# A transformer block in split 16-bit products: one pass of attention scores with DMA transposes in place of two passes

## The chip, the cores and the metric

The kernel runs on one core of one Trainium2 chip. The metric is the device time of one execution in microseconds (us), lower is better. A core has five engines that run beside each other, each in the order of its own instruction list: TensorE (PE, matrix products into PSUM, with weight loads shown as PEld), VectorE (DVE), ScalarE (ACT), GpSimd (POOL) and SyncE (SP), which here issues nearly all DMAs. They wait for one another through semaphores.

## The reference

```python
# x: (16, 512, 512); 16 heads of 32; INTER = 1408
xn = _layernorm(x)
def attn(x):
    qkv = jnp.einsum('bsd,ed->bse', x, w_qkv) + b_qkv           # q, k, v by heads
    scores = jnp.einsum('bhqd,bhkd->bhqk', q, k) / math.sqrt(Hd) + causal
    out = jnp.einsum('bhqk,bhkd->bhqd', jax.nn.softmax(scores), v)
    return jnp.einsum('bsd,ed->bse', out, w_out) + b_out
def ffn(x):                                                      # ternary weights with scales
    g = jnp.einsum('th,ih->ti', x, gate_w) * gate_s
    u = jnp.einsum('th,ih->ti', x, up_w) * up_s
    return jnp.einsum('ti,hi->th', jax.nn.silu(g) * u, down_w) * down_s
return x + attn(xn) + ffn(xn)
```

The ternary weights hold only -1, 0 and 1. All tensors are float32.

## The kernel before

A batch row has 512 tokens by 512 features. It is worked on in tiles of 128 partitions by 512: four token blocks (tb) or four feature chunks (kc). Float32 products are made from 16-bit ones: a value is split into a high and a low float16 half after an exact scaling, and high by high, high by low and low by high are summed in PSUM. Ternary weights need no split; they lie in SBUF as float16 (wg, wu, wd).

Attention goes by slots. A slot is a group of four heads of one row, so there are 16 x 4 = 64 slots. Two passes over the scores are made. The first (`s1_step`, L354 to L369) computes a head's 128 queries by all keys up to them, in PSUM tile s; VectorE takes the row maximum with the causal mask (L363, negm), and ScalarE the exponential in place, only for its row sum (L369, den). `s1_fin` then turns maxima and denominators into pieces of float16 (pc), transposes them on TensorE (mT, L409) and sends the maxima by a DMA into rows 96 to 98 of the query tile QS (L405). The second pass (`s2_step`) computes the scores again, this time with keys on partitions, with 99 rows so that the maximum is already subtracted (L426): ScalarE takes the exponential (p, L441), GpSimd zeroes what is above the diagonal (L436), ScalarE and VectorE write the high and low halves ph (L443) and pl (L446). These are the moving operands of the value products (`av_step`, L461), which are made in four places of the slot, one for each key block, each with three groups of four matmuls: one matmul a head, 32 columns of TensorE's array each. `av_fin` spreads the reciprocal denominators over partitions by four matmuls (R, L483), scales the result and splits it into oh and ol.

The dense products fill TensorE between these steps. A `Fill` lays them out evenly over a slot: the query and key projections two slots ahead (`qk_proj`), the transposes of the next row's norm (`ln_tr`, L276), the gate and up chunks (`ffn_chunk`), the value projection (`v_proj`), the down projection (`down_tile`) and the output projection of the row before (`out_tile`). They share `mm_group` (L213).

The order is written out by hand: `at(time, function)` gives every step a planned time in us, and `run_events` emits the steps sorted by it. TensorE and SyncE issue in exactly that order; the planned times order the work and say nothing of how long it takes. `qk_place` (L316) has six DMAs a slot, which copy the halves of queries and keys from (dim, head) partitions into QS and KS, of which there are two sets each. PSUM's eight banks are three for the dense products (mm), two for the first scores (s1), two for the second (s2), and one for the value products (av).

```python
    def place():
        nc.vector.tensor_copy(mT(), ps()[:80, :P])
        nc.sync.dma_start(QSt[slot][96:99].rearrange("p j (i c) -> p (j i) c", i=4), mT()[32:80])
```

## Time and profile before

| what | value |
|---|---|
| median of 3 runs | 2243.9 us (2239.43 to 2244.49) |
| span of the profiled execution, first to last instruction | 2242.9 us, 1.0 us under that median |
| busy: PE, DVE, ACT, POOL | 2161.9, 1768.9, 1646.2, 1004.2 us |
| granted TensorE clock, mean | 0.996 |
| DMA, mean over the span | 54 GB/s, 122.04 MB in all |
| share of 16 DMA engines, queue of SyncE and ScalarE | 21.6% |

The page of a profile has the busy time of each engine, the span in 40 slices (each digit a tenth of the slice), the DMA queues, the chain of work that ended last, and groups of instructions: line, engine, operation, output and inputs, count, busy time, mean in ns, and then the idle time of the engine just before them with what ended it. In the timeline a line begins with its start and its duration in us. SPq is SyncE's queue: the duration there is that of the issue, not of the transfer.

### The profile page before, as it was taken

What the parts mean: (1) busy time and instruction counts of PE and PEld (TensorE: products, weight loads), DVE (VectorE), ACT (ScalarE), POOL (GpSimd) and SP (SyncE); (2) the same over time, 40 slices, a digit from 0 to 9 for tenths busy, and PEclk for the clock granted to TensorE, in tenths of its full rate; (3) what the DMA queues carried; (4) which work ended last, traced back from release to release, by engine and by line L of the source; (5) the groups of instructions that cost most, each with busy time, mean ns of one, the idle gap of its engine ahead of it and who ended that gap; (6) DMA issues with size and microseconds to landing.
All of it is one profiled execution on the core that took longest, in us unless ns stands there. A gap on an engine that the chain in (4) does not pass through costs nothing.

```text
span 2242.9 us, 39079 instructions
## 1 busy us (share of the span) xinstructions
PE 2161.9 (96%) x12994; PEld 964.2 (43%) x12994; DVE 1768.9 (79%) x4748; ACT 1646.2 (73%) x4145; POOL 1004.2 (45%) x1299
## 2 busy tenths in 40 slices
PE   5899999999999999999999999999999999999998
PEld 2434444444444444444444444444444444444433
DVE  7887869788787877879778697887978878787774
ACT  4877868778677777767777687786777877777773
POOL 5444353543534444344443534435344353544434
PEclk9999999999999999999999999999999999999999
DMA  8122131121221222222222211213212222122111
GB/s 195 34 48 67 34 72 51 31 67 47 63 56 29 67 52 53 56 44 58 47 62 48 68 43 38 72 39 71 54 28 67 53 57 53 40 52 44 40 38 40
DMA packets 99251, 122.04 MB, mean 54 GB/s; under 512 B 13920, under 2 KB 68576, under 8 KB 99040
## 3 DMA queue, kind: packets, MB, share of 16 engines
q1 hardware_dynamic: 94416, 115.14, 21.6%
q0 software_dynamic: 4624, 4.33, 1.2%
q8 instruction: 104, 1.70, 0.3%
q14 instruction: 107, 0.88, 0.1%
HBM read 55.85 MB, written 16.78 MB: 32 GB/s over the span
## 4 chain that ended last, share of the span: by engine, by line
PE 48%; DVE 17%; ACT 16%; DMA 6%; POOL 6%; issue 4%; SPq 1%; POOLq 0%; ACTq 0%; DVEq 0%
PE u L213 7%; PE g L213 7%; PE v L213 6%; PE dn L213 5%; ACT s L369 5%; PE op L213 5%; PE av L461 5%; PE qk L213 5%; DMA xr<-in_x 4%; ACT ph L443 4%; PE s L354 4%; ACT p L441 4%; DVE pl L446 3%; PE s L426 3%; DVE s L363 3%
## 5 line engine op out<-in xcount | busy, mean ns | idle before, releaser
L446 DVE SCALAR_TENSOR_TENSOR pl<-p,ph 128x512 f16<-128x512 f32 (+1 forms) x704 | 530.6, 757 | 139.2 <-ACT ph L443 135.7
L369 ACT ACTIVATE s<-s,negm 128x128 f32<-128x128 f32 (+3 forms) x1024 | 514.8, 503 | 170.7 <-DVE negm L363 163.9
L363 DVE CUSTOM_DVE_ANT_0 s<-s,mask 128x128 f32<-128x128 f32 (+3 forms) x1024 | 501.9, 492 | 118.0 <-PE s L354 116.2
L436 POOL TENSOR_SCALAR_AFFINE_SELECT p<-p 128x128 f32<-128x128 f32 (+2 forms) x704 | 304.0, 433 | 617.4 <-ACT p L441 589.3
L443 ACT ACTIVATE ph<-p 128x512 f16<-128x512 f32 (+1 forms) x704 | 416.0, 595 | 128.6 <-POOL p L436 125.5
L441 ACT ACTIVATE p<-s 128x512 f32<-128x512 f32 (+1 forms) x704 | 394.5, 561 | 58.3 <-PE s L426 56.0
L354 PE MATMUL s<-KS,QS 96*128 96x128 f16 (+3 forms) x1024 | 308.1, 301 | 50.9 <-ACT s L369 36.7
L519 POOL TENSOR_TENSOR hl<-ft,hh 128x512 f16<-128x512 f32 x176 | 216.8, 1232 | 236.7 <-ACT hh L518 236.5
L213 PE MATMUL u<-xh,wu 128*128 128x512 f16 x704 | 268.4, 381 | 0.0
L213 PE MATMUL g<-xh,wg 128*128 128x512 f16 x704 | 267.9, 381 | 0.0
L213 PE MATMUL dn<-wd,hh 128*128 128x512 f16 x704 | 267.6, 380 | 0.0
L213 PE MATMUL g<-xl,wg 128*128 128x512 f16 x704 | 267.1, 379 | 0.0
L213 PE MATMUL u<-xl,wu 128*128 128x512 f16 x704 | 266.8, 379 | 0.0
L213 PE MATMUL dn<-wd,hl 128*128 128x512 f16 x704 | 266.2, 378 | 0.0
L426 PE MATMUL s<-QS,KS 99*128 99x512 f16 (+3 forms) x1024 | 255.1, 300 | 0.5 <-DMA QS<-mTs 0.5
L369 ACT ACTIVATION_READ_ACCUMULATOR s<-s,negm 128x1 f32 x1024 | 209.7, 205 | 0.0
L213 PEld LDWEIGHTS <-wu 128*128 128x128 f16 x1408 | 126.4, 97 | 156.5 <-issue 31.2
L213 PEld LDWEIGHTS <-wg 128*128 128x128 f16 x1408 | 130.4, 98 | 143.1 <-issue 16.1
L306 POOL TENSOR_TENSOR qkl<-qkt,qkh 128x512 f16<-128x512 f32 x128 | 156.9, 1226 | 64.6 <-DVE qkh L305 52.5
L354 PEld LDWEIGHTS <-QS 96*128 96x128 f16 x1024 | 99.8, 97 | 140.1 <-issue 40.0
L518 ACT CAST hh<-ft 128x512 f16<-128x512 f32 x176 | 108.0, 614 | 59.7 <-DVE ft L516 57.9
L213 PEld LDWEIGHTS <-wq_h 128*128 128x128 f16 x1024 | 97.2, 97 | 122.8 <-issue 15.9
(131 smaller groups left out, 3508.0 us busy)
## 6 DMA issues: line engine op xcount, KB each, us to landing
xc<-in_x SPq DMA_DIRECT2D x64, 256.0 KB
QS<-qkh SPq DMA_DIRECT2D x128, 128.0 KB
KS<-qkh SPq DMA_DIRECT2D x128, 128.0 KB
xr<-in_x SPq DMA_DIRECT2D x64, 256.0 KB
out<-y SPq DMA_DIRECT2D x64, 256.0 KB
QS<-qkl SPq DMA_DIRECT2D x64, 128.0 KB
KS<-qkl SPq DMA_DIRECT2D x64, 128.0 KB
wq<-in_wqkvP SPq DMA_DIRECT2D x12, 256.0 KB
```

The lines of the kernel that those rows point to most:

```text
L213: nc.tensor.matmul(ps(), l, r, start=(k == 0), stop=(k == n - 1))
L306: f.after(1.8, lambda: nc.gpsimd.tensor_tensor(l(), t(), h(), ALU.subtract))
L354: nc.tensor.matmul(ps()[:, :n], QSt[slot][0:96, j, i * P : (i + 1) * P], KSt[slot][0:96, j, 0:n], start=True, stop=True,)
L363: last["rowmax"] = nc.vector.tensor_tensor_reduce(ps()[:, :n], ps()[:, :n], mask[:, 512 - n :], -(2.0 ** -7), 3e38, ALU.add, ALU.min, d["n ...
L369: nc.scalar.activation(ps()[:, :n], ps()[:, :n], AF.Exp, bias=d["negm"]()[:, c : c + 1], scale=-1.0, accum_out=d["den"]()[:, c : c + 1],)
L426: nc.tensor.matmul(ps()[:, u * n : (u + 1) * n], KSt[slot][0:KROW, j, kb * P : (kb + 1) * P], QSt[slot][0:KROW, j, kb * P : 512], start=Tr ...
L436: nc.gpsimd.affine_select(dg, dg, [[0, len(js)], [1, P]], ALU.is_ge, 0.0, base=0, channel_multiplier=-1)
L441: at(when + 0.35, lambda: nc.scalar.activation(p32()[:, :w], ps()[:, :w], AF.Exp, scale=2.0 ** -7))
L443: at(when + 1.5, lambda: nc.scalar.mul(ph()[:, :w], p32()[:, :w], 2.0 ** 15))
L446: lambda: nc.vector.scalar_tensor_tensor(pl()[:, :w], p32()[:, :w], 2.0 ** 15, ph()[:, :w], ALU.mult, ALU.subtract),
L461: nc.tensor.matmul(d["av"]()[j * 32 : (j + 1) * 32, kb * P : 512], st[b][vn]()[:, kb, f : f + 32], d[("p", kb, j)][pi](), start=(kb == 0 a ...
L519: f.after(2.0, lambda: nc.gpsimd.tensor_tensor(hl(), t(), hh(), ALU.subtract))
```

## The change

The scores are computed once. `score_pair` takes two heads and one query block: each head's scores go into one of four PSUM banks (s1), the row maximum and the exponential in place follow as before, and now the exponentials are kept. VectorE takes the reciprocals of the two row sums, GpSimd scales them, ScalarE writes the high half of the normalized weights from PSUM (`high`) and VectorE the low half (`low`), both into pq in SBUF, queries on partitions. One DMA transpose on SyncE (`turn`) puts all 128x128 blocks of the pair (4, 8, 12 or 16) with keys on partitions into pT, of which there is one set. The value products of a group are one run of 72 matmuls in the next slot, `AV_LAG` = 7.0 us of planned time after its start, and `av_fin` only splits their result. The second score pass, the pieces of maxima, the spread and the causal select are gone, and with them the rows 96 to 98.

The norm's rows are split into halves with tokens on partitions (ScalarE, GpSimd) and put on feature partitions by two DMA transposes a token block, in place of TensorE transposes. The query and key projections run one slot ahead instead of two. The ternary weights lie in SBUF as one-byte floats. A slot's planned length is the dense work + 4.4 instead of + 7.4.

```diff
-    QSt = [cp.tile([P, 4, 512], F16, name=f"QS{n}") for n in range(NS)]
-    KSt = [cp.tile([P, 4, 512], F16, name=f"KS{n}") for n in range(NS)]
-    for n in range(NS):
-        # rows 96..98 = 2^13, 2^2, 2^-9
-        nc.gpsimd.memset(KSt[n][96:99], 2.0 ** -9)
-        nc.gpsimd.memset(KSt[n][96:98], 4.0)
-        nc.gpsimd.memset(KSt[n][96:97], 8192.0)
+    QSt = [cp.tile([96, 4, 512], F16, name=f"QS{n}") for n in range(NS)]
+    KSt = [cp.tile([96, 4, 512], F16, name=f"KS{n}") for n in range(NS)]
+    pT = [
+        cp.tile([P, 2, 4, 2, 2, 256], F16, name="pT23"),
+        cp.tile([P, 2, 2, 2, 2, 256], F16, name="pT01"),
+    ]
...
-    wg = cp.tile([P, KC, I], F16, name="wg")
-    wu = cp.tile([P, KC, I], F16, name="wu")
-    wd = cp.tile([P, IC, D], F16, name="wd")
+    wg = cp.tile([P, KC, I], F8, name="wg")
+    wu = cp.tile([P, KC, I], F8, name="wu")
+    wd = cp.tile([P, IC, D], F8, name="wd")
...
     def ln_norm(b, tb):
         s = st[b]
         xc = s["xs"][tb]
+        if tb == 0:
+            s["xh"] = wk.tile([P, KC, 512], F16, tag="xh", name=f"xh_{b}", bufs=2)
+            s["xl"] = wk.tile([P, KC, 512], F16, tag="xl", name=f"xl_{b}", bufs=2)
+        h = wk.tile([P, 512], F16, tag="xnh", name=f"xnh_{b}_{tb}", bufs=1)
+        l = wk.tile([P, 512], F16, tag="xnl", name=f"xnl_{b}_{tb}", bufs=1)
         nc.vector.tensor_scalar(
             xc, xc, s["mv"][:, tb, 0:1], s["rstd"][:, tb : tb + 1], ALU.subtract, ALU.mult
         )
-    def ln_tr(f, b, kc):
+        nc.scalar.copy(h, xc)
+        nc.gpsimd.tensor_tensor(l, xc, h, ALU.subtract)
+        s[("xn", tb)] = h, l
+    def ln_tr(b, tb):
         s = st[b]
-        ps = Lazy(lambda: mm(f"lnT_{b}_{kc}"))
-        def tr():
-            if kc == 0:
-                s["xh"] = wk.tile([P, KC, 512], F16, tag="xh", name=f"xh_{b}", bufs=2)
-                s["xl"] = wk.tile([P, KC, 512], F16, tag="xl", name=f"xl_{b}", bufs=2)
-            for tb in range(NT):
-                nc.tensor.transpose(
-                    ps()[:, tb * P : (tb + 1) * P], s["xs"][tb][:, kc * P : (kc + 1) * P], ident
-                )
-        f.pe(0.45, tr)
-        f.after(0.3, lambda: nc.scalar.copy(s["xh"][:, kc, :], ps()))
-        f.after(1.0, lambda: nc.vector.tensor_tensor(s["xl"][:, kc, :], ps(), s["xh"][:, kc, :], ALU.subtract))
...
+    def score_pair(when, gap, b, g, i, pr):
         slot = (b * NG + g) % NS
         n = (i + 1) * P
+        nm = f"{b}_{g}_{i}_{pr}"
+        den = Lazy(lambda: wk.tile([P, 2], F32, tag="den", name="den_" + nm, bufs=4))
+        r = Lazy(lambda: wk.tile([P, 2], F32, tag="r", name="r_" + nm, bufs=4))
+        pq = Lazy(lambda: wk.tile([P, 4, 2, 2, P], F16, tag="pq", name="pq_" + nm, bufs=3))
+        pss = []
+        def score(ps, j):
             nc.tensor.matmul(
                 ps()[:, :n],
+                QSt[slot][:, j, i * P : (i + 1) * P],
+                KSt[slot][:, j, 0:n],
                 start=True,
                 stop=True,
             )
+        def rowmax(ps, negm):
             last["rowmax"] = nc.vector.tensor_tensor_reduce(
+                ps()[:, :n], ps()[:, :n], mask[:, 512 - n :], -(2.0 ** -7), 3e38, ALU.add, ALU.min, negm()
             )
+        def expo(ps, negm, u):
             nc.scalar.activation(
+                ps()[:, :n], ps()[:, :n], AF.Exp, bias=negm(), scale=-1.0, accum_out=den()[:, u : u + 1]
             )
+        def recip():
+            nc.vector.reciprocal(r(), den())
+            nc.gpsimd.tensor_scalar(r(), r(), 2.0 ** 15, None, ALU.mult)
+        def half(u):
+            return [pq()[:, 0 : i + 1, u, z, :] for z in range(2)]
+        def high(ps, u):
+            nc.scalar.mul(half(u)[0], ps()[:, :n].rearrange("p (k q) -> p k q", q=P), r()[:, u : u + 1])
+        def low(ps, u):
+            h, l = half(u)
+            nc.vector.scalar_tensor_tensor(
+                l, ps()[:, :n].rearrange("p (k q) -> p k q", q=P), r()[:, u : u + 1], h, ALU.mult, ALU.subtract
+            )
+        def turn():
+            dst = pT[0 if i > 1 else 1][:, pr].rearrange("p k u z q -> p (k u z) q")
+            src = pq().rearrange("p k u z q -> p (k u z q)")
+            nc.sync.dma_start_transpose(
+                dst[:, 0 : 4 * (i + 1), (i % 2) * P : (i % 2 + 1) * P], src[:, 0 : 4 * n]
+            )
+        for u in range(2):
+            t = when + gap * u
+            ps = Lazy(lambda u=u: pp.tile([P, 512], F32, tag="s1", name=f"s1_{nm}_{u}", bufs=4))
+            negm = Lazy(lambda u=u: wk.tile([P, 1], F32, tag="negm", name=f"negm_{nm}_{u}", bufs=6))
+            pss.append(ps)
+            at(t, score, ps, 2 * pr + u)
+            at(t + 0.35, rowmax, ps, negm)
+            at(t + 0.7 + 0.001 * n, expo, ps, negm, u)
+        at(t + 1.3 + 0.002 * n, recip)
+        for u in range(2):
+            w = t + 1.8 + (0.002 + 0.001 * u) * n + 0.2 * u
+            at(w, high, pss[u], u)
+            at(w + 0.3 + 0.001 * n, low, pss[u], u)
+        at(t + 2.5 + 0.005 * n, turn)
...
+    def av_step(when, b, g):
         d = grp[(b, g)]
+        def run():
+            for side, k0 in ((0, 0), (1, 0), (0, 1), (1, 1), (0, 2), (0, 3)):
+                q0 = P if (side == 0 and k0 == 3) or (side == 1 and k0 == 1) else 0
+                col = 0 if side else 256
+                for x, (vn, z) in enumerate((("vh", 0), ("vl", 0), ("vh", 1))):
+                    for j in range(4):
+                        f = g * P + j * 32
+                        nc.tensor.matmul(
+                            d["av"]()[j * 32 : (j + 1) * 32, col + q0 : col + 256],
+                            st[b][vn]()[:, k0, f : f + 32],
+                            pT[side][:, j // 2, k0, j % 2, z, q0:256],
+                            start=(side == 0 and k0 == 0 and x == 0),
+                            stop=(k0 == 3 and x == 2),
+                            skip_group_check=True,
+                        )
+        at(when, run)
...
     def av_fin(when, b, g):
         d = grp[(b, g)]
         nm = f"{b}_{g}"
-        R = Lazy(lambda: pp.tile([P, 512], F32, tag="s2", name="R_" + nm, bufs=2))
-        r = Lazy(lambda: tmp32("Rs_" + nm, "r32", 1))
         oh = Lazy(lambda: wk.tile([P, 512], F16, tag="oh", name="oh_" + nm, bufs=5))
         ol = Lazy(lambda: wk.tile([P, 512], F16, tag="ol", name="ol_" + nm, bufs=5))
-        def spread():
-            for i in range(4):
-                nc.tensor.matmul(R()[:, i * P : (i + 1) * P], sel[:, i, :], d["rT"], start=True, stop=True)
-        at(when - 1.3, spread)
-        at(when - 0.9, lambda: nc.scalar.copy(r(), R()))
+        at(when, lambda: nc.scalar.mul(oh(), d["av"](), 2.0 ** -15))
         at(
-            when + 0.3,
-            lambda: nc.vector.scalar_tensor_tensor(r(), d["av"](), 2.0 ** -24, r(), ALU.mult, ALU.mult),
-        )
-        at(when + 1.2, lambda: nc.scalar.copy(oh(), r()))
-        at(when + 1.9, lambda: nc.gpsimd.tensor_tensor(ol(), r(), oh(), ALU.subtract))
+            when + 0.7,
+            lambda: nc.vector.scalar_tensor_tensor(ol(), d["av"](), 2.0 ** -15, oh(), ALU.mult, ALU.subtract),
+        )
         st[b][("o", g)] = (oh, ol)
...
     def attention_slot(s, t0, T):
+        if s > 0:
+            b, g = divmod(s - 1, NG)
+            at_av = t0 + AV_LAG
+            av_step(at_av, b, g)
+            av_fin(at_av + 2.2, b, g)
+        if s < NSLOT:
+            b, g = divmod(s, NG)
+            grp[(b, g)] = dict(
+                av=Lazy(lambda: pp.tile([P, 512], F32, tag="av", name=f"av_{b}_{g}", bufs=1)),
+            )
+            unit = T / (4 * sum((i + 1) * P + 150 for i in range(4)))
+            t = t0
+            for i in (3, 2, 1, 0):
+                gap = ((i + 1) * P + 150) * unit
+                for pr in range(2):
+                    score_pair(t, gap, b, g, i, pr)
+                    t += 2 * gap
...
+    AV_LAG = 7.0
     for s in range(NSLOT):
         b, g = divmod(s, NG)
         f = fillers(s)
-        T = f.total + 7.4
+        T = f.total + 4.4
         attention_slot(s, start, T)
         f.place(start, T)
...
-                at(start + T * (0.79 + 0.06 * tb), late, ln_norm, b + 1, tb)
+                at(start + T * (0.8 + 0.2 * tb), late, ln_norm, b + 1, tb)
+                at(start + T * (0.8 + 0.2 * tb) + 4.0, ln_tr, b + 1, tb)
```

## The prediction

> **What bounds the kernel now.** I read the shares of busy time, then the slices, the groups, the timeline of two stretches and the chain.
>
> ```profile
> span 2242.9 us, 39079 instructions
> PE 2161.9 (96%) x12994; PEld 964.2 (43%) x12994; DVE 1768.9 (79%) x4748; ACT 1646.2 (73%) x4145; POOL 1004.2 (45%) x1299
> PE   5899999999999999999999999999999999999998
> PEclk9999999999999999999999999999999999999999
> ```
>
> TensorE has 81 us of idle in the whole span, most of it in the first two slices, at a full clock. So its stream of matmuls is the bound, and work taken out of it is worth its own length, as long as nothing else becomes longer. The groups show the second score pass and what hangs on it:
>
> ```profile
> L446 DVE SCALAR_TENSOR_TENSOR pl<-p,ph 128x512 f16<-128x512 f32 (+1 forms) x704 | 530.6, 757 | 139.2 <-ACT ph L443 135.7
> L436 POOL TENSOR_SCALAR_AFFINE_SELECT p<-p 128x128 f32<-128x128 f32 (+2 forms) x704 | 304.0, 433 | 617.4 <-ACT p L441 589.3
> L443 ACT ACTIVATE ph<-p 128x512 f16<-128x512 f32 (+1 forms) x704 | 416.0, 595 | 128.6 <-POOL p L436 125.5
> L441 ACT ACTIVATE p<-s 128x512 f32<-128x512 f32 (+1 forms) x704 | 394.5, 561 | 58.3 <-PE s L426 56.0
> L426 PE MATMUL s<-QS,KS 99*128 99x512 f16 (+3 forms) x1024 | 255.1, 300 | 0.5 <-DMA QS<-mTs 0.5
> ```
>
> A matmul's mean there is longer than its turn, since matmuls overlap. The turn is the distance between two starts in the timeline:
>
> ```profile
> 1001.17 0.38 PE L213 MATMUL dn<-wd,hh 128*128 128x512 f16 x1
> 1001.39 0.38 PE L213 MATMUL dn<-wd,hl 128*128 128x512 f16 x1
> ...
> 1006.65 0.39 PE L483 MATMUL R<-mTs,sel 32*128 32x128 f16 x4
> 1006.97 0.25 PE L409 MATMUL mT<-ident,pc 128*80 128x128 f16 x1
> 1007.06 0.38 PE L213 MATMUL dn<-wd,hh 128*128 128x512 f16 x1
> ```
>
> 512 columns take 0.216 us, the reciprocal spread (R) 0.32, the transposed maxima (mT) 0.09. SyncE's queue, on which the new work lands, is seen in the full timeline:
>
> ```profile
> 58.59 0.87 SPq L405 DMA_DIRECT2D QS<-mTs  x1
> ...
> 60.99 0.38 PE L426 MATMUL s<-QS,KS 99*128 99x512 f16 x1 [0.54 <-DMA QS<-mTs]
> ```
>
> From the start of an issue to its reader 2.4 us pass, so some 1.5 after the issue. The placements of queries and keys (L316) hold the queue 0.55 to 0.61 us each, the loads of x 0.46 (four in 1.84).
>
> In the chain, the same step of a row (the load of xc behind the norm) recurs at 361.42 and ten rows later at 1728.37: 136.7 us a row, 34.2 a slot of four heads. 64 slots are 2187, the two ends 56. The profiled span is 1.0 us under the median of the runs, 2243.9; I add that at the end.
>
> [...] The trace holds no transpose by DMA and no one-byte matmul[...].
>
> **The change, part by part, per slot.**
>
> TensorE. Gone: the second scores, 4 x (0.216 + 0.167 + 0.11 + 0.055) = 2.2 us (turns of 512, 384, 256 and 128 columns at L426); R and mT 0.41; the norm's transposes, four in 0.44 to 0.50 us, 1.9 a row, 0.5 a slot. The value products (L461): now twelve groups of four in four places, each entered and left with 0.1 us lost; the four stretches I measured are 1.30, 0.97, 0.73 and 0.58 = 3.6 us. Then 18 groups in one run: 12 of 256 columns at 0.12 and 6 of 128 at 0.07, plus one switch 0.2, = 2.1. Saved 1.5. Together 4.6 us, 294 in all: 2161.9 falls to 1868, 29.2 a slot.
>
> VectorE. Gone: pl 530.6, the eight steps on maxima and denominators 107.5, the copy of mT 13.8, the norm's xl 43.8. Added: 1024 low halves from PSUM; by the nearest PSUM rows (688 ns for 512; 559, 424 and 294 from the row maxima) 256 x 1.965 = 503; 512 reciprocals between 0.15 and 0.25 us, taken 0.2: 102. The weight checks lose 27 reductions and gain 35, nothing. 1769 becomes 1678, 26.2 a slot: below TensorE, though not by much.
>
> ScalarE. Gone: 394.5 + 416.0 + 37.4 (copy of R). Added: 1024 high halves at 598, 495, 392 and 289 ns (p's two shapes, then their slope): 454. 1646 becomes 1252, 19.6 a slot, free. GpSimd: minus 304.0 (causal) and 75.0 (ol), plus 64 norm halves at 1.23 and 512 small products of 0.1 to 0.2: about 770, 12 a slot. But each small product now stands between a pair's exponentials and its high halves, and can sit behind one 1.23 us subtraction.
>
> SyncE, the part that decides. A group turns 2 x (4+3+2+1) x 4 = 80 blocks of 128x128[...], in eight DMAs[...]. Six placements at 0.59: 3.5; loads and stores 12 a row at 0.45: 1.4; weight checks 0.2. Sum 29.1 us in a slot in which TensorE needs 29.2. Gone is QS<-mTs, 0.76. The data themselves are 2.9 MB a slot[...]. [...]
>
> The new wait: pT is single. A group's first transpose waits until the value products of the group before have read pT, and those wait for that group's last transpose. Behind the waiting transpose SyncE holds the placements, loads and stores; behind them stand the next slot's scores (KS, QS). So a cycle is the queue's 29.1, plus 1.5 us until the last transpose has landed, plus 2.1 of products, less some 0.6 of loads or norm transposes that fit between: 32.1 us. That is 3 us over TensorE's stream, which the 4.6 saved pay for.
>
> One-byte weights: no time on TensorE; half the start-up load of 4.3 MB on the software queue, hidden behind the first row. Ends: the norm's halves now go through DMA at the start (+3), the last products wait for their transposes (+3), the first norm transposes (4.1) and the second projection (5.2) leave the start: 53 to 55. Sum: 64 x 32.1 + 55 = 2109, and 1 around the span: **2110 us**.
>
> **The rivals.**
>
> The transpose costs more a tile (slower). Break-even is 34.2 us a slot[...]. It would show as TensorE waiting in one block per slot for pT, or for KS.
>
> The four score banks (slower or level). A score tile now stays in PSUM from its matmul to its low half: at 512 columns 0.22 + 0.83 + 0.86 + 0.2 + 0.15 + 0.6 + 0.69 = 3.6 us plus the pair's second tile, and waits on a VectorE that is over 80% busy. Eight pairs through two places break even at 8.5 us a pair; I reckon 5 to 7. If this decides, 2250 to 2400.
>
> The queue is not the limit (faster still). [...] TensorE has 29.2 and about 1.3 us of waits: 64 x 30.5 + 55 = 2007; with no new wait at all 1925.
>
> That the change does not do what it says has nothing for it: the removed passes are gone from the code.
>
> **How the numbers follow.** The queue as summed, 2010 to 2230: 0.35. Queue not the limit, 1950 to 2010: 0.12. Within 0.3%, 7 us, which is what measurements of this kernel can tell from no change: 0.05. Dearer tiles 0.36, of which I leave 0.15 beyond 3300. Banks 0.12. Faster 0.47, same 0.05, slower 0.48: the sign is nearly open, since the forecast lies 130 us from the break-even of a price that no row shows. The likeliest case alone spans 2010 to 2230; the range that holds 8 in 10 goes from 1970 to 3300.
>
> **What would show it.** Right: no L426, R, mT or lnT in the groups; 29 us of TensorE stream a slot; SPq nearly full with transposes[...]; TensorE's idle some 3 us a slot, released by a DMA into pT. Wrong: a 16-block transpose of over 4.5 us from issue to issue (dearer tiles), idle of scores behind DVE pq (the banks), or TensorE at 96% again (the queue hidden).

## The result, and the profile after

The changed kernel takes 2335.24 us (median of 4 runs, 2322.34 to 2340.42) against 2242.07 us for the kernel before: 1.0407 times as long, 95% interval 1.0375 to 1.0439. The forecast was 2110 us and faster. The profiled execution took 2340.42 us, with a span of 2338.6. The page of the profile after, busy time and slices:

```profile
span 2338.6 us, 39976 instructions
PE 1978.5 (85%) x12930; PEld 926.2 (40%) x12930; DVE 1683.9 (72%) x4945; ACT 1408.0 (60%) x3697; POOL 775.2 (33%) x1101
PE   1978888988889888898888889898798898898886
PEclk9999999999999999999998999999999999999998
DMA  8567688788686787777786776876767777776774
```

No engine is full any more. TensorE, at 96% before, has 360 us of idle, spread over all slices, and a longer start (the first digit is 1, before it was 5). VectorE and GpSimd came out within 6 us of the prediction's sums (1678 and 770). The groups of the page say what TensorE waits for (after the bar: busy time and mean; then the idle time before the group, and what ended most of it):

```profile
L347 PE MATMUL s<-KS,QS 96*128 96x512 f16 (+3 forms) x1024 | 316.6, 310 | 279.1 <-DVE pq L377 278.0
L373 ACT ACTIVATE pq<-s,r 128x512 f16<-128x512 f32 (+3 forms) x1024 | 483.3, 524 | 297.9 <-POOL r L367 226.3
L471 POOL TENSOR_TENSOR xr<-xr,bo_b 128x512 f32<-128x512 f32 x64 | 81.2, 1269 | 198.2 <-DMA xr<-in_x 192.8
L205 PE MATMUL qk<-xh,wq_h 128*128 128x512 f16 x512 | 146.5, 412 | 47.4 <-DMA xh<-xnh 47.4
```

Read them as one chain. A score needs a PSUM bank, and a bank is free when VectorE has made the low half (L377). That waits for ScalarE's high half (L373), which waits for GpSimd's product of the reciprocal (L367). Ahead of some products in GpSimd's list stands the residual add L471, which has 198 us of idle, nearly all for the load of xr. The 278 us there are what the prediction named as the sign of the bank rival. The fourth line is the start: TensorE waits 47.4 us for the first norm rows.

The length of a slot is taken from the first score of one slot to that of the next. A row's four slots take 37.2, 33.8, 34.6 and 35.8 us after (means over slots 4 to 59), together 141.4; before, the same stretches of dense work (there they run beside the scores of the group after) take 35.5, 33.3, 34.4 and 33.4, together 136.6. So the slots cost 64 x (35.35 - 34.14) = 77 us more, and the two ends 19 more (76 against 58). The predicted 2109 had 32.1 a slot and 55.

One place where the chain is late, in the timeline of the kernel after, in slot 3 (the down projection); a line has its start, its duration, and in brackets the idle time before it with what ended it:

```profile
1039.40 0.54 SPq L470 DMA_DIRECT2D xr<-in_x  x1
...
1040.89 0.15 DVE L366 RECIPROCAL r<-den 128x2 f32<-128x2 f32 x1
...
1044.70 1.26 POOL L471 TENSOR_TENSOR xr<-xr,bo_b 128x512 f32<-128x512 f32 x1 [5.65 <-DMA xr<-in_x]
1045.93 0.21 POOL L367 TENSOR_SCALAR r<-r 128x2 f32<-128x2 f32 x1
1046.17 0.84 ACT L373 ACTIVATE pq<-s,r 128x256 f16<-128x256 f32 x2 [4.13 <-POOL r L367]
1046.68 0.88 DVE L377 SCALAR_TENSOR_TENSOR pq<-s,r,pq 128x256 f16<-128x256 f32 x2 [3.48 <-ACT pq L373]
1047.22 0.22 PE L347 MATMUL s<-KS,QS 96*128 96x128 f16 x1 [3.30 <-DVE pq L377]
```

The reciprocal is there at 1041.0; the product of 0.21 us comes at 1045.93, because the add before it waits for a load issued at 1039.40 that lands 5 us later. ScalarE, VectorE and at last TensorE stand. What this costs beside the 3.3 us is in the same kernel's busy time by stretches (busy us of PE, PEld, DVE, ACT, POOL, each with its count; granted clock, DMA share, GB/s):

```profile
1044.00:1048.00 4.00, 0.78 (x4) 0.31 (x4) 1.24 (x5) 1.34 (x5) 2.87 (x4) 0.92 0.41 85
1048.00:1052.00 4.00, 4.00 (x16) 1.75 (x15) 1.60 (x8) 2.19 (x9) 1.60 (x3) 0.65 1.03 219
```

After the gap TensorE is busy for all of the next 4 us, at a mean clock of 0.65. The clock records of the trace show half rate for 238.6 us in all after, and 19.6 before. All 46 half-rate stretches of after begin on one grid of 3.41 us, and nearly all last one or two of its steps (3.41 or 6.83 us). In the 3.41 us before these stretches TensorE is idle for 1.9 to 3.4 us (3.2 in the one shown), in one gap or in several: before the stretch at 1832.5 us there are two, of 1.00 and 0.86 us. The steps after the first score that no half rate follows have 2.0 us of idle at most. In the kernel before two of the three stretches follow a wholly idle step, and the third (at 2163.9 us) one with 1.33 us of idle, so the traces show no sharp limit. Part of the 1978.5 us of busy TensorE in after is slow work: it is busy in 197 of the 238.6 us, and there the dense 512-column matmuls start 0.427 us apart in place of 0.216 (medians), so about half of that, 99 us, is lost, which leaves 1880 where the prediction's sum was 1868.

### The profile page after: what moved, and what is told of

Read it like the earlier page. It is cut to its first block, busy times and chain, and to the rows that moved or that the text cites. A ratio compares the mean times of both kernels' runs of the same rounds, so it can differ in the third digit from the quotient of the medians.

```text
span 2338.6 us, 39976 instructions
## 1 busy us (share of the span) xinstructions
PE 1978.5 (85%) x12930; PEld 926.2 (40%) x12930; DVE 1683.9 (72%) x4945; ACT 1408.0 (60%) x3697; POOL 775.2 (33%) x1101
## 4 chain that ended last, share of the span: by engine, by line
PE 37%; DVE 24%; DMA 18%; ACT 6%; issue 6%; SPq 4%; POOL 4%; ACTq 0%; POOLq 0%; DVEq 0%
PE qk L205 11%; DMA pT<-pq 8%; DVE pq L377 7%; PE dn L205 6%; DMA xr<-in_x 5%; PE v L205 5%; DVE s L356 4%; PE u L205 4%; PE s L347 4%; PE g L205 4%; PE av L415 3%; ACT pq L373 3%; SPq L307 2%; DVE ft L459 2%; DVE ft L455 2%
## 5 line engine op out<-in xcount | busy, mean ns | idle before, releaser
L361 ACT ACTIVATE s<-s,negm 128x512 f32<-128x512 f32 (+3 forms) x1024 | 516.3, 504 | 362.2 <-DVE negm L356 313.6
L377 DVE SCALAR_TENSOR_TENSOR pq<-s,r,pq 128x512 f16<-128x512 f32 (+3 forms) x1024 | 524.8, 545 | 207.8 <-ACT pq L373 206.6
L373 ACT ACTIVATE pq<-s,r 128x512 f16<-128x512 f32 (+3 forms) x1024 | 483.3, 524 | 297.9 <-POOL r L367 226.3
L356 DVE CUSTOM_DVE_ANT_0 s<-s,mask 128x512 f32<-128x512 f32 (+3 forms) x1024 | 503.3, 493 | 218.6 <-PE s L347 213.6
L347 PE MATMUL s<-KS,QS 96*128 96x512 f16 (+3 forms) x1024 | 316.6, 310 | 279.1 <-DVE pq L377 278.0
L367 POOL TENSOR_SCALAR r<-r 128x2 f32<-128x2 f32 x512 | 110.5, 216 | 620.5 <-DVE r L366 550.2
L205 PE MATMUL dn<-wd,hh 128*128 128x512 fp8e4 x704 | 283.9, 403 | 0.0
L205 PE MATMUL dn<-wd,hl 128*128 128x512 fp8e4 x704 | 281.9, 400 | 0.0
L205 PEld LDWEIGHTS <-wu 128*128 128x128 fp8e4 x1408 | 135.9, 98 | 200.7 <-issue 61.3
L205 PE MATMUL qk<-xh,wq_h 128*128 128x512 f16 x512 | 146.5, 412 | 47.4 <-DMA xh<-xnh 47.4
L471 POOL TENSOR_TENSOR xr<-xr,bo_b 128x512 f32<-128x512 f32 x64 | 81.2, 1269 | 198.2 <-DMA xr<-in_x 192.8
L205 PE MATMUL qk<-xl,wq_h 128*128 128x512 f16 x512 | 146.1, 412 | 0.0
```

What stands on the lines that cost most here:

```text
L205: nc.tensor.matmul(ps(), l, r, start=(k == 0), stop=(k == n - 1))
L347: nc.tensor.matmul(ps()[:, :n], QSt[slot][:, j, i * P : (i + 1) * P], KSt[slot][:, j, 0:n], start=True, stop=True,)
L356: last["rowmax"] = nc.vector.tensor_tensor_reduce(ps()[:, :n], ps()[:, :n], mask[:, 512 - n :], -(2.0 ** -7), 3e38, ALU.add, ALU.min, negm())
L361: nc.scalar.activation(ps()[:, :n], ps()[:, :n], AF.Exp, bias=negm(), scale=-1.0, accum_out=den()[:, u : u + 1])
L367: nc.gpsimd.tensor_scalar(r(), r(), 2.0 ** 15, None, ALU.mult)
L373: nc.scalar.mul(half(u)[0], ps()[:, :n].rearrange("p (k q) -> p k q", q=P), r()[:, u : u + 1])
```

## The experiments

A table first; the sections below refer to it. Medians in us, the ratio to the kernel before with its 95% interval, the start of the first score, the length of a row's slots 0 to 3, and the time at half clock, the last three from the trace of the profiled execution.

| kernel | median | ratio | first score | slots 0, 1, 2, 3 | half clock |
|---|---|---|---|---|---|
| before | 2242.07 | 1 | 37.7 | 35.5, 33.3, 34.4, 33.4 | 19.6 |
| after | 2335.24 | 1.0407 (1.0375 to 1.0439) | 68.8 | 37.2, 33.8, 34.6, 35.8 | 238.6 |
| e1_mul_dve | 2364.41 | 1.0542 (1.0524 to 1.0559) | 70.3 | 38.8, 34.6, 33.3, 35.9 | 225.7 |
| e2_one_block | 2235.11 | 0.9952 (0.9935 to 0.9970) | 68.9 | 35.7, 30.7, 32.7, 35.8 | 159.5 |
| e3_ln_pe | 2269.77 | 1.0117 (1.0100 to 1.0134) | 45.2 | 38.2, 32.5, 32.2, 35.7 | 157.6 |
| e4_before_fp8 | 2251.83 | 1.0045 (1.0031 to 1.0060) | 35.9 | 36.5, 33.3, 34.4, 33.3 | 12.8 |
| e5_norm_slot3 | 2213.17 | 0.9870 (0.9854 to 0.9887) | 44.6 | 32.8, 31.6, 32.2, 37.5 | 101.1 |
| e6_xr_two | 2292.07 | 1.0217 (1.0200 to 1.0234) | 70.4 | 36.5, 33.6, 34.3, 34.4 | 208.4 |
| e7_both | 2231.51 | 0.9956 (0.9939 to 0.9973) | 45.5 | 32.8, 31.6, 32.3, 38.2 | |
| e8_both_mul_dve | 2243.80 | 1.0012 (1.0000 to 1.0025) | 45.6 | 33.9, 31.7, 32.6, 37.4 | |
| e9_add_late | 2232.12 | 0.9960 (0.9947 to 0.9974) | 45.9 | 33.2, 31.6, 32.2, 38.3 | |
| e10_after_add_late | 2297.31 | 1.0250 (1.0229 to 1.0271) | 69.5 | 36.2, 33.3, 33.9, 34.5 | |
| e11_heads_close | 2443.05 | 1.0891 (1.0869 to 1.0912) | 45.9 | 38.0, 34.7, 37.2, 39.5 | |
| e12_residual_early | 2163.42 | 0.9655 (0.9637 to 0.9672) | 45.5 | 32.6, 31.5, 31.2, 35.7 | 82.4 |
| e13_heads_close_2 | 2118.32 | 0.9456 (0.9440 to 0.9472) | 45.5 | 32.8, 30.6, 31.3, 33.8 | 78.9 |
| e14_after_residual_early | 2306.25 | 1.0293 (1.0267 to 1.0318) | 69.3 | 39.1, 35.4, 32.3, 32.6 | 202.5 |
| e15_after_heads_close | 2301.66 | 1.0262 (1.0245 to 1.0279) | 67.4 | 36.7, 34.0, 33.7, 34.6 | 207.5 |
| e16_heads_closer | 2091.10 | 0.9326 (0.9310 to 0.9342) | 45.0 | 32.4, 30.2, 31.0, 33.2 | 51.3 |
| e17_norm_by_dma | 2158.51 | 0.9623 (0.9601 to 0.9644) | 70.4 | 34.9, 29.2, 31.3, 33.7 | 87.6 |
| e18_best_one_block | 2063.13 | 0.9201 (0.9182 to 0.9220) | 41.9 | 32.6, 29.7, 30.9, 32.0 | 46.2 |

My theories: A, GpSimd's link in the chain behind an add that waits for its load; B, the transposes' data and landing, through pq and pT; C, SyncE's list, held by waits of its own; later D, VectorE full in slot 0; and the bank rival of the prediction, the time that a bank is held.

### First four: one part each

e1_mul_dve takes GpSimd out of the chain:

```diff
-            nc.gpsimd.tensor_scalar(r(), r(), 2.0 ** 15, None, ALU.mult)
+            nc.vector.tensor_scalar(r(), r(), 2.0 ** 15, None, ALU.mult)
```

> The scale product of a pair's reciprocals goes from GpSimd to VectorE; nothing else changes. Theory A (GpSimd's link in the chain: the product stands behind the residual add, which waits 5 us for its load, so the score banks come free late): the wait from reciprocal to product, 5.0 us on average for the fifth pair of a down-projection slot and 0.1 to 1.4 elsewhere, falls to under 0.3 everywhere; TensorE's idle before scores falls from 4.3 to about 2.5 us a slot, its half-clock time from 239 to under 150 us, and the time to 2170 to 2260. Theory B (the transposes end last, through pq and pT): under 20 us of change. Theory C (SyncE's order): under 40.

It lost another 29 us. Slot 0 rose by 1.6 us, and slot 3 kept its length, though TensorE's idle in it fell from 5.1 to 3.4 us. In slot 0 VectorE was already busy 32.8 us of 37.2 in the kernel after, and the product on it costs: TensorE's idle there rose from 6.2 to 8.5 us. So the GpSimd link alone is not the loss.

e2_one_block leaves attention weights out: only the first 128x128 block of each transpose moves.

```diff
-                dst[:, 0 : 4 * (i + 1), (i % 2) * P : (i % 2 + 1) * P], src[:, 0 : 4 * n]
+                dst[:, 0:1, (i % 2) * P : (i % 2 + 1) * P], src[:, 0:P]
```

> Every pair's transpose turns only its first 128x128 block instead of 4, 8, 12 or 16, and the rest of pT stays zero, so most of the attention weights are left out of the value products. The number of DMAs and all waits stay. Theory B (data or landing of the transposes set the pace): the DMA share falls from 72% to about 25% and the time to 2000 to 2150. Theory A: the load of the residual lands earlier on an emptier queue (3 us instead of 5), which shortens GpSimd's wait; 2230 to 2310. Theory C: 2250 to 2330, since SyncE's list and its waits are the same.

100 us came back, in slots 1, 2 and 0, none in slot 3. But not all waits stayed, as I had expected: the first block is the first head's high half alone, so the transposes start 0.7 us before the pair's last low half is made, on average, where they start 1.5 us after it in the kernel after. The 100 us are thus the price of the data and of that wait together, and even so the kernel is only level with the one before.

e3_ln_pe turns the norm's rows on TensorE again, with the functions of the kernel before.

> The norm's rows are transposed on TensorE and split from PSUM as in the kernel before; the rest is the changed kernel. Gone are 128 DMA transposes, and the waits of SyncE's list for the norm's halves. Theory C (SyncE's list is held up by the norm's transposes in slots 1 and 2 of a row, and the start by single buffers): start 35 us shorter, first score at some 35 us instead of 69, lag from low half to transpose in the second slot of a row from 3 to 5 us to under 1.5; time 2240 to 2290 in spite of 0.5 us a slot more on TensorE. Theories A and B: only the start, 2290 to 2310.

65 us came back: 23.6 at the start (first score at 45.2 instead of 68.8), and 1.3 and 2.4 us in slots 1 and 2, less 1.0 lost in slot 0. In slot 1 of the kernel after, a finished low half waits 2.7 to 5.3 us for its transpose in five of the eight pairs, with transposes of the norm in SyncE's list between them; in e3 it is at most 2.3.

e4_before_fp8 puts only the one-byte weights, with the kernel's own tests of their values, into the kernel before.

> The kernel before with the ternary weights in one byte, and nothing else of the change. If one-byte operands stream and load as two-byte ones do, as the prediction had it: within 0.3% of 2242, and dn, g and u at 380 ns a matmul. If they were slower on TensorE (the dn matmuls of the changed kernel have a mean of 403 ns against 380): 20 ns on 1408 of them would be 28 us, 2270.

The matmuls kept their length (g 379 ns where before has 381, u 381 and dn 380 as in before, weight loads 97), so the narrow weights brought TensorE no gain here and no harm. The 10 us are real, since the interval excludes 1. They lie in slot 0, which takes 36.5 us instead of 35.5 (14 us over all rows of the traces), less some 6 at the two ends; what lengthens it stays open.

### Slot 0: VectorE is full

The busy time of the kernel after in the four slots of one row, columns as before:

```profile
911.67:948.92 37.25, 30.93 (x208) 14.73 (x208) 33.41 (x96) 24.52 (x64) 13.64 (x19) 1.00 0.74 136
948.92:983.25 34.33, 27.63 (x194) 13.10 (x192) 25.78 (x76) 22.33 (x61) 10.43 (x17) 0.99 0.90 164
983.25:1018.32 35.07, 33.48 (x208) 15.39 (x208) 25.96 (x76) 22.66 (x60) 11.97 (x17) 0.91 0.68 114
1018.32:1053.35 35.03, 30.43 (x200) 14.34 (x200) 20.71 (x64) 17.96 (x50) 12.35 (x16) 0.95 0.64 114
```

VectorE has 33.4 us in slot 0 and 20.7 in slot 3: six gate and up chunks and most of the norm of the next row lie in the one, nothing of either in the other. e5_norm_slot3 takes e3 and moves the norm, with its loads of x.

```diff
-        if g == 0 and b + 1 < NB:
-            at(start, ln_load, b + 1)
+        nxt = 1 if s == 0 else b + 2 if g == 3 and b + 2 < NB else 0
+        if nxt:
+            at(start, ln_load, nxt)
...
```

> The kernel of e3_ln_pe with VectorE's norm steps (statistics, reciprocal root, normalization) of a row done one slot earlier: in slot 3 of the row two before it instead of slot 0 of the row before it. Theory D, VectorE is the bound of slot 0: it is busy 33.5 us there in a slot of 38.2, and some 6.5 us of that leave, while slot 3 has only 20.9 of 35.7. So slot 0 falls to 34 to 35.5 us, slot 3 stays within 0.7, and the total falls by 15 x 3 to 4 us, from 2270 to 2210 to 2225. Rival A, the chain of hand-overs sets the pace of every slot whatever VectorE's load: slot 0 keeps over 37 us and the total is 2260 to 2280. Rival E, the work only moves the wait: slot 3 grows by as much as slot 0 loses, 2260 to 2280 with slot 3 over 38.

57 us less, and below the kernel before. The same four slots in e5:

```profile
857.42:889.89 32.47, 30.32 (x208) 14.61 (x208) 26.97 (x76) 24.66 (x65) 12.48 (x18) 1.00 0.79 127
...
953.54:990.58 37.04, 31.86 (x200) 14.66 (x200) 26.48 (x89) 17.93 (x50) 12.42 (x16) 0.91 0.73 138
```

Slot 0 went from 38.2 to 32.8 on average, more than expected, and slot 3 grew by 1.8, which I had put at 0.7 at most. Theory D holds for slot 0. Slot 3, at 37.5, is not full on any engine.

### Slot 3: a load ahead of a product

e6_xr_two gives xr two buffers in the kernel after; e7_both gives them to e5; e8_both_mul_dve moves the product to VectorE as well.

```diff
-        xr = Lazy(lambda: wk.tile([P, 512], F32, tag="xr", name=f"xr_{b}_{tb}", bufs=1))
+        xr = Lazy(lambda: wk.tile([P, 512], F32, tag="xr", name=f"xr_{b}_{tb}", bufs=2))
```

> The kernel after with two buffers for the residual rows xr instead of one (a scratch tile of the start shares another's place to make room), so that a load of xr no longer waits for the add that reads the one before it. Theory A, in slot 3 GpSimd's reciprocal product waits about 5 us behind the residual add that waits for that load, and SyncE's list is held by the load: the delay from the reciprocal to its product in the fifth pair falls from 5.0 to under 1.5 us, slot 3 falls from 35.8 to about 33.5, and the total by 16 x 2.3 = 37 to about 2300 (2285 to 2315). Rival B, the transposes' landing keeps pq's three buffers taken: the wait goes on to pq, slot 3 stays above 35.3, 2325 to 2345.

> The kernel of e5_norm_slot3 with two buffers for xr. If theories A and D hold and their places are separate, the gains add: 2270 - 52 - 37 = about 2180 (2160 to 2200), slots all at 33 to 34.5 us. If slot 3, which now carries VectorE's norm steps too, is bound by something else (the landing of transposes through pq), only e5's part comes: 2210 to 2225.

> The kernel of e7_both with the product of the reciprocals on VectorE in place of GpSimd. If GpSimd's link still delays the chain when nothing long stands before it (0.22 us of work and two hand-overs), the slots fall by up to 8 x 0.2 = 1.6 us: 20 to 90 us under e7_both. If VectorE is again the bound where the gate and up chunks are (as in e1_mul_dve, where it cost 29 us), 15 to 35 us above e7_both.

e6 took 43 us off, near the forecast, but not for the reason given. The fifth pair's product still waits 4.9 us; what fell is the time from low half to transpose (in the fourth pair from 7.1 to 1.7 us): SyncE no longer holds the transposes behind a load that waits for its buffer. That is theory C, but the runs do not show that it accounts for the 43 us. TensorE's idle did not fall in slot 3 (5.1 and 5.2 us); it fell in the slot 0 that follows, from 6.2 to 4.2, of which 0.7 is waiting for pT. And in e7 the same edit took the fourth pair's time from 6.9 to 1.4 us, and nothing was gained over e5: 18 us were lost, TensorE's idle in slot 3 rose from 6.4 to 7.7, and the product still waits 4.7 us. Why the edit helps one kernel and not the other stays open. e8 lost 12 more. With the product off GpSimd TensorE's idle in slot 3 fell from 7.7 to 5.7 us, as in e1, but in slot 0 it rose from 2.2 to 5.0.

e9_add_late and e10_after_add_late put the add directly before its use in the program.

```diff
-        f.after(5.8, lambda: nc.gpsimd.tensor_tensor(xr(), xr(), bo_b, ALU.add))
...
+        f.after(1.2, lambda: nc.gpsimd.tensor_tensor(xr(), xr(), bo_b, ALU.add))
```

> The kernel of e7_both with the residual row's bias add on GpSimd put directly before the add that uses it, after the down projection's group, in place of ahead of it. In e7_both slot 3 takes 38.2 us and the reciprocal product of the fifth pair still waits 4.7 us: two buffers let the load go out, but the add stands ahead of the product in GpSimd's list and waits 5.4 us for the load to land. Theory A: with the add late the load has landed by then; that delay falls under 1.5 us, TensorE's idle in slot 3 from 7.7 to under 4 us, slot 3 to 33 to 35, and the total by 16 x 3.2 to 5 us, from 2231 to about 2165 (2150 to 2185). Rival B, slot 3 is held by transposes landing or by VectorE with the norm's steps (27.6 us): slot 3 stays above 36.5, 2205 to 2235.

> The same late add, and two buffers for xr, in the kernel after with nothing else changed. Theory A: slot 3 falls from 34.4 (e6_xr_two) to 32.5 to 33.5 since VectorE has only 20.5 us there; slots 0 to 2 stay at 36.5, 33.6 and 34.3; total 2292 - 16 x 1 to 2 = about 2268 (2255 to 2280). Rival C, what e6_xr_two gave was SyncE's list alone and the product's link is hidden by it: 2285 to 2295.

Both stayed where they were (e9 within 1 us of e7, e10 5 us above e6). GpSimd's order is not the planned one: outside the start, planned times order only TensorE and SyncE, and the scheduler put the add ahead of the product as before. The product waited 4.7 and 4.9 us. The mechanism had not been tested.

e12_residual_early loads xr a tile earlier and orders GpSimd by the planned times too; e14_after_residual_early does the same in the kernel after.

```diff
+        if tb == 0:
+            f.after(0.0, load, 0)
+        if tb + 1 < NT:
+            f.after(3.2, load, tb + 1)
...
-    with tc.manual_schedule(engines={ET.PE, ET.SP}):
+    with tc.manual_schedule(engines={ET.PE, ET.SP, ET.Pool}):
```

> The kernel of e9_add_late with each residual row loaded one tile earlier (two buffers) and GpSimd's list in the planned order, so that its add finds the load landed. In e9 the product of the fifth pair of slot 3 still waits 4.7 us: the scheduler had kept the add ahead of it. Theory A: that delay falls under 1.5 us, GpSimd's idle before xr from 142 us in all to under 30, slot 3 from 38.3 to 33 to 35, the total from 2232 to 2150 to 2185. Rival B, slot 3 is held by transposes landing in pT and pq or by VectorE's 27.6 us of work: the delay falls but slot 3 stays above 36.5, 2205 to 2235.

> The kernel after with the early load, the late add, two buffers and GpSimd's list in the planned order, nothing else. Theory A: the 5 us before the fifth pair's product in slot 3 go, slot 3 falls from 34.4 (e6_xr_two) to 32 to 33.5 as VectorE has only 20.5 us there, slots 0 to 2 stay (36.5, 33.5, 34.2): 2292 - 16 x 1 to 2.4 = 2255 to 2276. Rival C, once SyncE's list is freed by two buffers the product's wait costs nothing more: 2285 to 2297.

In e12 the product of the fifth pair waits 0.12 us instead of 4.7, slot 3 falls by 2.6 us (41 in 16 rows), and the total by 69 against e9. TensorE's idle in slot 3 falls from 7.8 to 5.8 us, as much as in e8. The other 28 us are not this wait: the edit orders the whole of GpSimd's list anew, and slot 2 fell by 1.0 and slot 0 by 0.6 as well. The early load and the new order are not tested apart. The idle of GpSimd before an add of xr, by the view of that tile, in e9 and then in e12 (us, times):

```profile
  DMA xr<-in_x: 141.9, 45
```

```profile
  DMA xr<-in_x: 31.9, 17
```

e14 missed: slot 3 fell to 32.6 as theory A says, but slots 0 and 1 rose by 2.6 and 1.9 us over e6, and the total by 14. The timeline of GpSimd in e14, slot 0, shows why:

```profile
1077.67 1.15 POOL L265 TENSOR_TENSOR xnl<-xc,xnh 128x512 f16<-128x512 f32 x1 [5.35 <-ACT xnh L264]
1078.79 0.21 POOL L367 TENSOR_SCALAR r<-r 128x2 f32<-128x2 f32 x1
```

Here the planned order puts the low half of the norm, which has to wait 5.35 us for ScalarE, ahead of a product. In the last three pairs of slot 0 the product waits 3.7 to 4.2 us on average; in e6 it waited 0.2. It is theory A at another place, made by my own edit. e12 has no such subtraction, since its norm is turned on TensorE.

### Banks: the two heads of a pair closer together

A bank is held from its score to its low half; the pair's second score was planned 2.8 us after the first in the widest blocks. e11_heads_close and e13_heads_close_2 plan it at 0.4 of that, e16_heads_closer at 0.1, e15_after_heads_close at 0.4 in the kernel after. All but e11 keep the transposes at their old times.

```diff
-            t = when + gap * u
+            t = when + 0.4 * gap * u
...
-        at(t + 2.5 + 0.005 * n, turn)
+        at(when + gap + 2.5 + 0.005 * n, turn)
```

> The kernel of e9_add_late with the second head's score of a pair planned 0.4 of a gap after the first instead of a whole gap (pairs keep their distance), so that a pair's two banks are filled close together. The rival that I had called the four score banks: a bank is held 8.5 to 9.7 us in the first two pairs of a slot, of which 2.8 to 4.7 us only wait for the second head. If the holding time sets TensorE's idle, it falls by 1.5 us in those pairs and the total by 64 x 0.5 to 1.5 us, 30 to 90 under e9_add_late. If VectorE and ScalarE's shares in the slot set it, the bunching costs or changes nothing: 10 under to 40 above e9_add_late.

> The kernel of e12_residual_early with the second head's score of a pair planned 0.4 of a gap after the first, the transposes left at their planned times (so that the value products keep their place ahead of the next group's transposes, which e11_heads_close had broken). If the time that a bank is held (8.5 to 9.7 us in the first pairs) sets TensorE's idle of 2 to 3 us in slots 0 and 1, the total falls by 64 x 0.5 to 1.5 = 30 to 90 us under e12. If VectorE's and ScalarE's share sets it: from 10 under to 40 above e12.

> The kernel after with one edit: the second head's score of a pair planned 0.4 of a gap after the first, transposes at their planned times. Bank rival: in after a pair's banks are held 7.9 us on average against two places for eight pairs in 35 us, and scores wait for the low half that frees a bank in all slots (279 us in all); the edit takes 1.5 to 2.5 us off the hold and the total falls by 40 to 90 us, to 2245 to 2295, in all four slots. Rival, the banks are only where other delays show (VectorE full in slot 0, GpSimd's product waiting in slot 3, SyncE held in slot 1): the delays stay and TensorE waits as long, 2315 to 2350.

> The kernel of e13_heads_close_2 with 0.1 of a gap in place of 0.4 between the two heads of a pair. If holding time still decides, 10 to 30 us under e13's 2118. If VectorE's and ScalarE's turn-taking decides by now (the second head's row maximum already waits 0.5 to 2 us for VectorE), within 8 of it or up to 20 above.

e11 says nothing on banks. Its first transpose of a group came ahead of the value products of the group before in the order, so these products read partly the new group's weights and TensorE waited for them. e13 gained 45 us and e16 another 27. The holding time of a pair, from first score to last low half, averages 7.9 us in after, 7.1 in e12, 6.3 in e13 and 6.2 in e16; TensorE's idle in slots 1 and 3 went from 3.0 and 5.8 (e12) to 0.9 and 3.7 (e16). The fall of the hold goes with e13's gain; from e13 to e16 the mean hold hardly changes, so what e16 gained is not shown to be holding time. In the kernel after alone (e15) the edit gave 34 us, less than forecast: the hold falls only to 7.4, and stays at 8.5 us in slot 0 and 7.8 in slot 1. The page of e16:

```profile
span 2088.1 us, 40214 instructions
PE 1928.9 (92%) x13186; PEld 939.2 (45%) x13186; DVE 1701.8 (82%) x5009; ACT 1390.3 (67%) x3697; POOL 707.4 (34%) x1037
PE   5988999999999999999999899999999999999987
L348 PE MATMUL s<-KS,QS 96*128 96x512 f16 (+3 forms) x1024 | 271.8, 302 | 108.2 <-DVE pq L378 105.3
```

The idle before scores is 108 us instead of 279. With 2091 us this kernel is 6.7% faster than the one before (ratio 0.9326, 0.9310 to 0.9342).

### What the transposes themselves cost in the end

e17_norm_by_dma puts the norm's DMA transposes back into e16; e18_best_one_block cuts the attention transposes in e16 to one block and so leaves weights out, as e2 did.

> The kernel of e16_heads_closer with the norm's rows turned by DMA again, as in the kernel after, in the slot to which the norm was moved. In after that part cost 65 us in all (e3_ln_pe): 23.6 at the start (first scores at 68.8 instead of 45.2), the rest in slot 1, where SyncE's list waits for the halves of the norm. Theory C: the start costs its 23 us again and slot 3, which now holds the norm's transposes beside the residual loads, 1 to 3 us each: 2091 + 23 + 15 to 45 = 2130 to 2160. Rival: TensorE's 1.9 us a row of transposes saved and no wait: 2091 + 23 - 25 = 2085 to 2105.

> The kernel of e16_heads_closer with each attention transpose cut to its first 128x128 block (pT is zeroed once; the weights of the other blocks are left out of the products). In after the same cut gave 100 us (e2_one_block). If the transposes' data and landing (theory B) still bind, 40 to 100 us under 2091. If what the cut gave in after was relief for waits that are gone by now, 2070 to 2095: little but the 2.7 us of TensorE's waits in slot 3 and 0.95 for the value products is left to win.

e17 cost 67 us: 25 at the start, as expected, and the rest mostly in slot 0 (2.5 us), where I had put it in slot 3: the planned times of the norm's blocks, 0.8 to 1.4 of a slot, carry three of the four into the next slot 0. The sum came as theory C has it, but the cause in the slots is not shown to be SyncE's list: with the norm's halves back on GpSimd, in planned order as in e14, the product of the reciprocals waits 2.6 us in the first pair of slot 0 and 1.8 in the third, where it waited 0.2 and 0.1 in e16. e18 gained 28 us, less than theory B's range has and just past its rival's. Some 3 of them are at the start, before any attention transpose (first score at 41.9 instead of 45.0). The median landing of a transpose fell from 4.1 to 2.2 us by it, as the issues by line show, e16 and then e18:

```profile
pT<-pq SPq DMA_TRANSPOSE x512, 4.1
```

```profile
pT<-pq SPq DMA_TRANSPOSE x512, 2.2
```

So nearly all data of the attention transposes, together with the wait for the last low half (as in e2, they start 0.7 us before it), are worth at most 28 us of 2091 once the chain has slack; in the kernel after, the same cut was worth 100.

## Why the prediction was wrong

The step that failed is the cycle of 32.1 us a slot: SyncE's queue of 29.1 us, held up by the single pT, was to set the pace. Of the 29.1 us only 5.1 (placements, loads and stores, weight checks) were summed from the trace of before; the price of the transposes was shown by no trace. In the trace of after all issues of SyncE together take 21.8 us of a slot of 35.3 (means over slots 4 to 59), and TensorE waits 0.3 us a slot for pT. In its place TensorE waits 278 us, 4.3 a slot, for a score bank. The bank comes free at the end of a chain over VectorE, ScalarE and GpSimd, and two delays of that chain had been put at nothing: a slot 0 in which VectorE is nearly full, and a GpSimd list that waits for a load. The range of 1970 to 3300 holds 2335, but it reaches that far up for dearer transposes, which did not come.

**TensorE's stream: right.** 1868 us predicted; 1978.5 measured, about 1880 without the time lost at half clock. In e16, busy for 42 us at half clock, 1929 less 21 and less the norm's transposes (64 slots of 0.5 us) is 1876.

**VectorE and GpSimd: the sums right, their use wrong; ScalarE 156 us too low.** ScalarE's sum took the groups that go off at their full busy time, 848 us; they overlap others on the engine, and without them the trace of before has only 656 us less. VectorE's sum made the same error on both sides (696 us taken off, 554 in the trace; 605 added, 482 in the trace), so that it came out right is luck. "26.2 a slot: below TensorE" is an average over slots of 32.8, 25.3, 26.0 and 20.9. Slot 0 had 32.0 us of VectorE before as well, in a slot of 35.5. A chain with VectorE in three of its links (row maximum, reciprocal, low half) comes late there, and the saved TensorE time brings nothing. e5 shows that this is worth 57 us.

**GpSimd's small product: a wait put at nothing.** I wrote that it "can sit behind one 1.23 us subtraction" and priced nothing. It sits behind whatever the list has before it, and that includes an add that waits for a DMA: 4.9 to 5 us on average in the fifth pair of slot 3. Taking the wait away takes 1.6 to 2.1 us off TensorE's idle in slot 3 (e1, e8, e12), some 30 us in 16 rows; e12's 69 us hold more than that. The kernel before has the same add, at L528, with 91.7 us of idle for its load; I did not ask what would stand behind it.

**SyncE, "the part that decides": mis-sized, and it did not decide.** A group's eight transposes were put too dear. Issues in the kernel after:

```profile
1026.97 1.80 SPq L384 DMA_TRANSPOSE pT<-pq  x1
1028.83 1.12 SPq L470 DMA_DIRECT2D xr<-in_x  x1
1033.22 1.48 SPq L384 DMA_TRANSPOSE pT<-pq  x1
...
1053.52 1.24 SPq L384 DMA_TRANSPOSE pT<-pq  x1
```

The medians by position in the slot are 1.98, 1.93, 1.49, 1.60, 1.28, 1.23, 1.20 and 1.20 us, together 11.9 (the means 13.1). From 4 blocks of 128x128 to 16 that is 0.75 us, 63 ns a block on average, though only some 0.05 us of it by 8. The price that I had taken does not fit this transpose, and the rival of dearer transposes (0.36), which was to show as over 4.5 us for 16 blocks where 1.9 to 2.0 were measured, fell with it. What SyncE did cost lay, as far as the runs show, in its order and not in its sum: transposes held behind loads that wait for the one buffer of xr (some part of e6's 43 us), and behind norm transposes that wait for their rows (part of e3's 65). Neither wait was in my list.

**The single pT: too dear.** I had 3 us of TensorE idle a slot for it. The value products wait 17.7 us for pT in the whole of after (23 times), 0.3 a slot:

```profile
  DMA pT<-pq: 17.7, 23
```

**The rival of four banks: its sign and size right, at 0.12.** It promised 2250 to 2400, a range that no sum led to, and idle of scores behind L377. Its price was a mean hold of 5 to 7 us against a break-even of 8.5. The mean is 7.9, below the break-even, and it loses all the same: by pair and slot the holds average between 4.2 and 10.9. That TensorE waits for the long ones and gets nothing back for the short ones is argued, not tested.

**The clock: not priced.** In after, half clock followed windows of 3.41 us with 1.9 us of idle or more, 239 us in all, and cost about 99 us of TensorE time.

**The ends: 55 predicted, 76.** I gave the norm's DMA 3 us. With one buffer for each half its eight transposes go one after the other, from 21.1 to 47.4 us; e3 takes 23.6 us off.

**One-byte weights at nothing:** right on TensorE (g, u and dn at 378 to 381 ns a matmul in e4), 10 us off in all.

**One reading that was wrong** and moved little: the first two slices hold 29 of the 81 us of TensorE's idle, not most of it.

## What to carry to other kernels

When work moves from TensorE into a chain over four engines that hands back a scarce buffer, the sum of each engine says little: price the chain at its slowest place, slot by slot, and ask for every link what stands ahead of it in its engine's list and what that waits for. Mean holding time under the break-even is not enough where the holds spread as here, from 4.2 to 10.9 us. Idle time that drops the clock is paid a second time in slow matmuls, here with about 99 us. A transform that looks lost can be repaired: four edits that change no arithmetic of the attention (norm rows on TensorE and in the slot with VectorE free, residual loads early with GpSimd in planned order, heads of a pair together) turned 1.041 into 0.933.

## What the runs showed of the hardware that I had not expected

- A DMA transpose within SBUF holds its queue for 1.2 us with 4 blocks of 128x128 and 1.9 to 2.0 with 16 (medians in after), and lands 2.4 us (least), 4.0 (median) or 7.9 (most) after the start of its issue, at a DMA share of 72%. With one block it lands after 2.2 us (median, e18).
- In after the granted clock fell to half on a grid of 3.41 us, after steps in which TensorE had been idle for 1.9 us or more, in one gap or in several; one of before's three stretches follows 1.33 us. After a gap of 3.3 us TensorE was busy through the next 4 us at a mean clock of 0.65.
- A 128x2 product on GpSimd takes 0.21 us; its place in the list cost up to 5.
